# Edge sums of a four-layer graph network: source weights in ScalarE's queue, an earlier folding of the last head's weights, another queue for layer 3's input

## The chip, the cores and the metric

The kernel runs on one NeuronCore of a Trainium2 chip. The metric is the device time of one execution in microseconds. The core has five engines with a queue each: TensorE (PE, matrix products, with its weight loads shown apart as PEld), VectorE (DVE), ScalarE (ACT), GpSimd (POOL) and SyncE (SP, which only issues transfers). Engines wait for each other through semaphores; each works its own queue strictly in order.

## The reference, cut to what matters

The reference is a network of four layers over a graph of 3125 nodes, 256 features each, and 50000 edges. Each layer adds a graph step and a mixer step of the normalized input to x, and then a feed-forward step. Layers 1, 2 and 3 use graph attention; layers 1 and 2 use it twice, with four heads and then with one.

```
def gat_layer(x, src, dst, W, a_src, a_dst, b, heads, out_ch, concat, n):
    h = (x @ W.T).reshape(n, heads, out_ch)
    alpha_src = jnp.sum(h * a_src, axis=-1)
    alpha_dst = jnp.sum(h * a_dst, axis=-1)
    e = jax.nn.leaky_relu(alpha_src[src] + alpha_dst[dst], NEG_SLOPE)
    ...
    out = jax.ops.segment_sum(alpha[:, :, None] * h[src], dst, num_segments=n)
    ...
    return out + b
```

Layer 3 has one attention with four heads of 64; its result is added to the layer's input and to a bias, before an ELU:

```
h_local = jax.nn.elu((agg + x.reshape(n, NH, FOUT)).reshape(n, NH * FOUT) + gat_b)
```

The kernel must compute all of this in float32, the selections of the feed-forward steps (top-k, experts) included.

## The kernel before, in words

**Tiles.** Nodes are cut into 25 tiles of 125 (`NT`, `P`). X, the running activations, stays on chip as 125 x 25 x 256. The edges are a dense matrix of 3125 x 3125 counts in DRAM (`adj`), built at the start; a row tile of it holds the edges of 125 source nodes.

**Edge sums.** `gat_products` runs five times: for the four heads of layer 1 (128 wide), the single last head of layer 1 (256 wide), the four heads of layer 2 (64 wide), its last head (256) and layer 3 (four heads of 64). `h` holds for each source tile and head the features and a one (`width + 1` columns, so that a product gives the sum of the weights too). The exponential of a leaky ReLU of a sum is written as a product of a factor of the source, `gpre`, and a maximum of two factors, `mine` (of the target) and `over` (of the source). So every source row is multiplied once by `gpre` (line 1099): 25 tensor products, of which POOL takes every third. Then the targets' `mine` is spread over the partitions by PE with an identity (`ps_spread`, line 174) and copied to `rows` by DVE (line 78) and ACT (line 80).

For heads of 128 or 256 the loop runs over five groups of five target tiles, and in each over the 25 source tiles `s`: the edges `a` come from `adj` (lines 800 and 801, two transfers issued by SP), DVE makes `t = max(rows, over) * a` for each head (line 1142), and PE multiplies it by `h[:, s]` into PSUM (line 1147). For heads of 64, `sums_by_feature` does the same with four columns of 7, 6, 6 and 6 target tiles; features are on the partitions there (DVE line 1218, PE lines 1223 and 1232), and ACT copies the sums at line 1240. What follows for a target tile is a generator, `use`: it divides by the sum of the weights (`shares`), adds the bias, applies the ELU, and for layers 1 and 2 multiplies by the weights of the last head. `use` runs one group or column behind, stepwise between source tiles.

**The last head's weights.** `gat_heads` loads `W2` (512 x 256 in layer 1, 256 x 256 in layer 2) into `w2a` and the bias into `b1`. `folded` multiplies `w2a` by the attention vectors and sums over features (lines 883 and 884), so that two more columns of `w2a` give the two attention terms of the last head: per layer four transfers on SP, and on DVE 8 + 8 operations in layer 1, 4 + 4 in layer 2. In the order of the program it stands after the layer's mixer, and right ahead of `gat`, whose first step, `gat_spans`, takes the extremes of the attention terms (`ext`, line 1038) and lets PE turn them (`ps_ext`, line 1046). Out of those come `over`, `mine` and `gpre`.

**The layer's input.** `layer_input` normalizes X group by group of four tiles to `XN` (DVE, line 138) and turns it with PE to `XNT`. The mixers read both. In layer 1 SP and ACT also zero two tables in DRAM (`f_rows`, `f_out`) at this time; in layer 2 the last step of the layer before, a gather of the experts' rows by POOL (line 2146) and 50 additions to X by DVE (line 1532), leads up to it. Each mixer begins with an addition of `XN` to X by POOL over the whole array.

**Layer 3.** The layer's input is read from DRAM as `local` (125 x 25 x 256, 3.1 MB) by two transfers issued by ACT (lines 800 and 801). In `l3_local` POOL adds the bias `gat_b` to all of `local` (line 1915), and `use` adds the attention's result to a tile of it (line 1920).

**Order.** A recording layer gathers all operations and orders them by itself before they go to the engines' queues; memory is given out by pools (`with self.pool(...)`), and an operation on a tile whose memory served something else waits for the last user of that memory. So the place of a pool in the program decides both, and a changed pool can move operations of others.

Of the kernel before, what the change touches and what calls it, by code (L numbers as in the profile page):

```python
# [11 lines left out]
F32 = mybir.dt.float32  # L12
BF16 = mybir.dt.bfloat16
I32 = mybir.dt.int32
AF = mybir.ActivationFunctionType
# [45 lines left out]
class Net:  # L61
# [1016 lines left out]
    def gat_products(self, far, h, al, heads, width, loops, use):  # L1078
# [3 lines left out]
        with ExitStack() as es:  # L1082
# [13 lines left out]
            nc.scalar.activation(mine, mine, AF.Exp, scale=-0.8)  # L1096
            for s in range(NT):
                eng = nc.gpsimd if s % 3 == 2 else nc.vector
                eng.tensor_mul(h[:, s], h[:, s], pre[:, s, :, None].to_broadcast([P, heads, width + 1]))
            if width < 96:  # L1100
                self.sums_by_feature(es, mine, over, h, heads, width, loops, use)
                return
# [20 lines left out]
            for g in range(NG):  # L1123
# [10 lines left out]
                for s in range(NT):  # L1134
                    a = ap.tile([P, GW], F32, name="a")
                    self.load_edges(a, self.adj_rows(), s, g)
                    if loops and s // GB == g:
                        blk = a[:, (s % GB) * P:(s % GB + 1) * P]
                        nc.vector.tensor_add(blk, blk, self.ident[:P, :P])
                    t = tp.tile([P, heads, GW], F32, name="t")  # L1140
                    for hd in range(heads):
# [19 lines left out]

    def sums_by_feature(self, es, mine, over, h, heads, width, loops, use):

# [34 lines left out]
        for i0, n in COLUMNS:  # L1198
# [10 lines left out]
            for s in range(NT):  # L1209
                a = ap.tile([P, most], F32, name="a")  # L1210
                self.halves(nc.sync, a[:, :w], self.adj_rows()[s * P:(s + 1) * P, i0 * P:i0 * P + w])
                if loops and i0 <= s < i0 + n:
                    blk = a[:, (s - i0) * P:(s - i0 + 1) * P]
                    nc.vector.tensor_add(blk, blk, self.ident[:P, :P])
                t = []
                for hd in range(heads):
# [84 lines left out]

    def gat_heads(self, prefix, h, al, h2, al2, heads, width, loops, eps):

        nc = self.nc
        wide = heads * width
        chunks = wide // 128
        h2v = h2[:, :, 0, :D]
        with ExitStack() as es:
            wp = es.enter_context(self.pool("tg_w"))
            kp = es.enter_context(self.pool("tg_k", 2))  # L1310
            w2 = wp.tile([128, chunks, D + 2], F32, name="w2a")
            nc.sync.dma_start(w2[:, :, :D], self.ins[prefix + "W2"].rearrange("(c p) m -> p c m", p=128))
            b1 = self.rows(wp, prefix + "b1")
            with self.pool("tg_f") as fp:
                self.folded(fp, w2[:, :, :D], chunks, 1, [prefix + "a_src2", prefix + "a_dst2"],
                            w2[:, :, D:])
            nc.gpsimd.memset(h2[:, :, :, D:D + 1], 1.0)
# [294 lines left out]
    def layer1(self):  # L1612
        self.rows1 = self.dram.tile([MAXB * BLK, D], F32, name="f1_rows")
        self.out1 = self.dram.tile([MAXB * BLK, D], F32, name="f1_out")
        self.blank(self.rows1, MAXB * BLK)
        self.blank(self.out1[OFTEN * BLK:, :], (MAXB - OFTEN) * BLK, 4)
        pre = "L1_gnn_"
        with self.pool("g1_h2") as low:
            last = self.last_terms(low)
            with self.pool("g1_h") as hp:  # L1620
                with self.pool("in1") as ip:
                    xn, xnt = self.layer_input(ip)
                    h, al = self.l1_mix(xn, xnt, lambda: self.gat_project(
                        hp, xnt, pre, "W1", 4, ("a_src1", "a_dst1"), "g1"))
                self.gat_heads(pre, h, al, *last, 4, 128, False, 1e-16)
            self.l1_ffn(lambda xn, xnt: self.gat_last(pre, *last, False, 1e-16, xn, xnt))
# [188 lines left out]
    def layer2(self):  # L1815
        pre = "L2_gnn_"
        with self.pool("g2_h2") as low:
            last = self.last_terms(low)
            with self.pool("g2_h") as hp:
                with self.pool("in2") as ip:  # L1820
                    xn, xnt = self.layer_input(ip)
                    h, al = self.l2_mix(xn, xnt, lambda: self.gat_project(
                        hp, xnt, pre, "W1", 4, ("a_src1", "a_dst1"), "g2"))
                self.gat_heads(pre, h, al, *last, 4, 64, True, 0.0)
            self.l2_ffn(lambda xn, xnt: self.gat_last(pre, *last, True, 0.0, xn, xnt))
# [67 lines left out]
    def l3_local(self, out, h, al, far, flag, most, found):  # L1893
# [4 lines left out]
        with ExitStack() as es:  # L1898
# [15 lines left out]

            nc.gpsimd.tensor_add(out, out, gb[:, None, :].to_broadcast([P, NT, D]))

            def use(pp, i, acc, eps):
                x = kp.tile([P, D], F32, name="agg")
                self.shares(kp, x, acc, 4, 64, less[:, i, :] if eps is None else eps)
                nc.vector.tensor_add(out[:, i, :], out[:, i, :], x)  # L1920
                yield from self.elu(kp, out[:, i, :], "elu")
# [231 lines left out]
    def l3_gnn(self):  # L2153
# [5 lines left out]
        with self.pool("in3_k") as keep:  # L2159
# [414 lines left out]
```

## Time and profile before

| | |
|---|---|
| median of 3 runs | 6754.28 us (6752.83 to 6755.14) |
| the profiled execution | 6747.62 us |
| its span, first to last instruction | 6745.8 us |
| mean granted clock of TensorE | 0.907 |
| DMA over the span | 562 MB, 83 GB/s |

Durations below are of the profiled execution. In a row of a timeline the first number is the start in us from the beginning of the span, the second the busy time; then come engine, line and operation, the tile written and those read, the shape, the number of instructions in the row, and in brackets how long the engine had been idle before it and whose signal came last before it went on. A row with the mark x17 takes 17 neighbouring instructions of one kind together. "PEld" overlaps PE. An engine's name with a q (ACTq, SPq) stands for its issuing of a transfer. A table of waits gives, for an engine's operation and the one that released it, the idle time in all, the number of times and the longest.

The start times of the five edge sums, from the first exponential `gpre` to the first product, are: layer 1's heads 1763.99 to 1782.86, layer 1's last 2437 to 2447.80, layer 2's heads 3726.86 to 3741.30, layer 2's last 4257 to 4267.69, layer 3's 5608.27 to 5617.96.

### The profile page before, as it was taken

The page shows a single profiled execution, that of the slowest core. Times are in us where ns is not written, and L with a number is a line of the kernel's source. Part 1 is how long each engine was busy: PE and PEld are TensorE (multiplying, and loading weights), DVE is VectorE, ACT ScalarE, POOL GpSimd, SP SyncE. Part 2 cuts the span into 40 slices and gives each one's busy share as a digit, 9 for nine tenths or more (in the row PEclk, how much of TensorE's full clock was granted, in tenths as well). Part 3 has the DMA queues.
Part 4 walks back from the last instruction along what each step waited for, and adds up shares of the span by engine and source line. Part 5 has one row for each costly group of instructions (what it writes and reads, how often), then busy time and mean ns, then how long its engine had stood idle before and what let it go on. Part 6 is the DMA issues. An engine that isn't in the chain of part 4 may idle for free. (4 is left out here: it accounts for less than half of the span.)

```text
span 6745.8 us, 78396 instructions
## 1 busy us (share of the span) xinstructions
PE 5820.6 (86%) x29487; PEld 3940.7 (58%) x29487; DVE 3700.8 (55%) x7628; ACT 1599.3 (24%) x3400; POOL 884.5 (13%) x685
## 2 busy tenths in 40 slices
PE   6888899997799989899956899898878887997785
PEld 5555785564699978658844344686534443333553
DVE  7634113215777754215025888546378888886433
ACT  2423002232011110113314011101256561003411
POOL 0000000002200001400031000111324452001101
PEclk7877998998899999889977899998889998998887
DMA  2633447501122234315520222440232223222132
GB/s 67 111 48 61 115 132 219 157 10 57 44 64 63 62 94 134 90 47 171 174 79 9 79 79 77 113 135 1 82 43 62 54 49 94 73 76 68 52 110 76
DMA packets 421342, 562.02 MB, mean 83 GB/s; under 512 B 120485, under 2 KB 307170, under 8 KB 417154
## 3 DMA queue, kind: packets, MB, share of 16 engines
q1 hardware_dynamic: 353687, 458.72, 25.8%
q10 hardware_dynamic: 40467, 70.52, 3.8%
q0 software_dynamic: 26752, 27.20, 1.6%
q8 instruction: 247, 4.05, 0.3%
q14 instruction: 189, 1.54, 0.1%
HBM read 446.41 MB, written 109.65 MB: 82 GB/s over the span
## 5 line engine op out<-in xcount | busy, mean ns | idle before, releaser
L1142 DVE SCALAR_TENSOR_TENSOR t<-rows,over,a 125x625 f32<-125x625 f32 x750 | 619.5, 865 | 423.3 <-PE acc L1147 416.0
L1218 DVE SCALAR_TENSOR_TENSOR t<-rows,over,a 125x750 f32<-125x750 f32 (+1 forms) x800 | 793.9, 1046 | 75.8 <-PE acc L1232 71.0
L1223 PE MATMUL acc<-t,g_h 125*64 125x375 f32 (+1 forms) x3200 | 596.0, 500 | 13.0 <-DVE t L1218 13.0
L1147 PE MATMUL acc<-g_h,t 125*125 125x129 f32 x5000 | 572.4, 274 | 6.3 <-ACT x L1273 3.5
L1147 PE MATMUL acc<-h,t 125*125 125x257 f32 x2500 | 556.7, 382 | 19.5 <-DVE t L1142 9.7
L1147 PEld LDWEIGHTS acc<-g_h,t 125*125 125x125 f32 x5000 | 563.7, 187 | 11.1 <-DVE t L1142 4.3
L1147 PEld LDWEIGHTS acc<-h,t 125*125 125x125 f32 x2500 | 466.2, 188 | 103.1 <-PE acc L1147 18.8
L1223 PEld LDWEIGHTS acc<-t,g_h 125*64 125x64 f32 x3200 | 219.7, 136 | 340.6 <-issue 239.1
L1232 PE MATMUL acc<-t,g_h 125*32 125x375 f32 (+1 forms) x3200 | 359.2, 496 | 0.0
L2093 POOL TENSOR_TENSOR bx<-h,crow 128x500 f32<-128x500 f32 (+1 forms) x224 | 263.7, 1195 | 306.2 <-issue 81.0
L779 PE MATMUL agg<-h,a 125*125 125x257 f32 x1250 | 278.8, 383 | 14.5 <-DMA a<-adj 9.3
L845 DVE SCALAR_TENSOR_TENSOR X<-ps_out,prob,X 125x256 f32<-125x256 f32 x200 | 87.9, 479 | 357.1 <-PE ps_out L166 356.9
L2099 PE MATMUL y<-bx,ident 128*128 128x500 f32 (+1 forms) x448 | 222.2, 610 | 67.4 <-POOL bx L2093 65.4
L779 PEld LDWEIGHTS agg<-h,a 125*125 125x125 f32 x1250 | 234.0, 189 | 57.7 <-issue 18.8
L2090 DVE TENSOR_TENSOR_SCAN h<-da,state,bx 128x500 f32<-128x500 f32 (+1 forms) x224 | 246.2, 1130 | 14.9 <-ACT da L2088 11.5
L569 ACT ACTIVATE h<-ps_hidden,L_ffn_b,bn_s 128x500 f32<-128x500 f32 (+1 forms) x224 | 160.7, 723 | 353.6 <-PE ps_hidden L166 333.5
L1232 PEld LDWEIGHTS acc<-t,g_h 125*32 125x32 f32 x3200 | 99.6, 109 | 237.0 <-issue 236.1
L166 PE MATMUL ps_hidden<-xbt,w 128*128 128x250 f32 x928 | 204.9, 379 | 16.2 <-ACT xbt L151 16.2
L166 PE MATMUL ps_out<-w,hb 128*125 128x256 f32 x928 | 205.0, 379 | 0.0
L166 PEld LDWEIGHTS ps_hidden<-xbt,w 128*128 128x128 f32 x928 | 174.6, 191 | 42.0 <-ACT xbt L151 23.1
L166 PE MATMUL ps_hidden<-XNT,L_ffn_W 128*128 128x500 f32 (+1 forms) x448 | 198.3, 567 | 0.0
L166 PEld LDWEIGHTS ps_out<-w,hb 128*125 128x125 f32 x928 | 174.1, 188 | 25.8
(724 smaller groups left out, 9332.1 us busy)
## 6 DMA issues: line engine op xcount, KB each, us to landing
a<-adj SPq DMA_DIRECT2D x500, 273.4 KB
a<-adj SPq DMA_DIRECT2D x150, 328.1 KB
arow<-adj SPq DMA_DIRECT2D x25, 1367.2 KB
adj<-block SPq DMA_DIRECT2D x22, 1531.2 KB
w<-in_L_ffn_W1p SPq DMA_DIRECT2D x29, 1024.0 KB
w<-in_L_ffn_W2p SPq DMA_DIRECT2D x29, 1024.0 KB
crow<-crows ACTq DMA_DIRECT2D x96, 250.0 KB
a<-adj SPq DMA_DIRECT2D x50, 382.8 KB
```

The source lines that it names most:

```text
L166: self.nc.tensor.matmul(ps, lhsT[k], rhs[k], start=(k == 0), stop=(k == n - 1))
L569: self.nc.scalar.activation(out[:, f, :], ps[:, :nt], func, **kw)
L779: nc.tensor.matmul(acc[b][:P, :D + 1], a[:, b * P:(b + 1) * P], h[:, s, :], start=(s == 0), stop=(s == NT - 1))
L845: nc.vector.scalar_tensor_tensor(x, ps, prob[:, g + j, e:e + 1], x, op0=ALU.mult, op1=ALU.add)
L1142: nc.vector.scalar_tensor_tensor(t[:, hd, :], rows[:, hd, :], over[:, s, hd:hd + 1], a, op0=ALU.max, op1=ALU.mult)
L1147: nc.tensor.matmul(acc(b, hd), t[:, hd, b * P:(b + 1) * P], h[:, s, hd, :], start=(s == 0 and first), stop=(s == NT - 1), skip_group_check ...
L1218: nc.vector.scalar_tensor_tensor(t[hd][:, :w], rows[hd][:, :w], over[:, s, hd:hd + 1], a[:, :w], op0=ALU.max, op1=ALU.mult)
L1223: nc.tensor.matmul(acc[k][c][q * width:(q + 1) * width, :c1 - c0], h[:, s, 2 * k + q, :width], t[2 * k + q][:, c0:c1], start=(s == 0), sto ...
L1232: nc.tensor.matmul(acc[pairs][c][hd * 32:(hd + 1) * 32, :c1 - c0], h[:, s1, hd, width:].to_broadcast([P, 32]), t1[hd][:, c0:c1], start=(s1 ...
L2090: nc.vector.tensor_tensor_scan(h[:, :w], da[:, :w], bx[:, :w], state[:, c, s:s + 1], op0=ALU.mult, op1=ALU.add)
L2093: nc.gpsimd.tensor_mul(bx[:, :w], h[:, :w], crow[:, :w])
L2099: nc.tensor.matmul(acc[c][:, :w], self.ident, terms[c][:, :w], start=(s == 0), stop=(s == S - 1))
```

## The change

Four things are changed.

1. The products by `gpre` are taken from DVE and POOL. A function `weigh(s)` does them for one source tile, head by head, as ACT activations (a copy scaled per partition). It is called in the loop over source tiles, in the first group or column alone, right before the edges are multiplied.
2. Loading and folding the last head's weights is a function of its own, `last_weights`. It is called at the beginning of layers 1 and 2, before `layer_input`, and its tiles live in the pool of `h` (`g1_h`, `g2_h`). In `gat_heads` the pool `tg_w` falls away.
3. `local` of layer 3 is loaded by POOL's queue.
4. The bias of layer 3 is added in `use`, by DVE, to the attention's result of each tile; POOL's addition to all of `local` is gone.

```diff
-            for s in range(NT):
-                eng = nc.gpsimd if s % 3 == 2 else nc.vector
-                eng.tensor_mul(h[:, s], h[:, s], pre[:, s, :, None].to_broadcast([P, heads, width + 1]))
+
+            def weigh(s):
+                for hd in range(heads):
+                    nc.scalar.activation(h[:, s, hd, :], h[:, s, hd, :], AF.Copy, scale=pre[:, s, hd:hd + 1])
             if width < 96:
-                self.sums_by_feature(es, mine, over, h, heads, width, loops, use)
+                self.sums_by_feature(es, mine, over, h, weigh, heads, width, loops, use)
                 return
...
+                    if g == 0:
+                        weigh(s)
                     t = tp.tile([P, heads, GW], F32, name="t")
...
+                if i0 == 0:
+                    weigh(s)
                 t = []
...
-    def gat_heads(self, prefix, h, al, h2, al2, heads, width, loops, eps):
+    def last_weights(self, pool, prefix, wide):
+
+        chunks = wide // 128
+        w2 = pool.tile([128, chunks, D + 2], F32, name="w2a")
+        self.nc.sync.dma_start(w2[:, :, :D], self.ins[prefix + "W2"].rearrange("(c p) m -> p c m", p=128))
+        b1 = self.rows(pool, prefix + "b1")
+        with self.pool("tg_f") as fp:
+            self.folded(fp, w2[:, :, :D], chunks, 1, [prefix + "a_src2", prefix + "a_dst2"], w2[:, :, D:])
+        return w2, b1
+
+    def gat_heads(self, weights, h, al, h2, al2, heads, width, loops, eps):
...
+        w2, b1 = weights
         with ExitStack() as es:
-            wp = es.enter_context(self.pool("tg_w"))
             kp = es.enter_context(self.pool("tg_k", 2))
-            w2 = wp.tile([128, chunks, D + 2], F32, name="w2a")
-            nc.sync.dma_start(w2[:, :, :D], self.ins[prefix + "W2"].rearrange("(c p) m -> p c m", p=128))
-            b1 = self.rows(wp, prefix + "b1")
-            with self.pool("tg_f") as fp:
-                self.folded(fp, w2[:, :, :D], chunks, 1, [prefix + "a_src2", prefix + "a_dst2"],
-                            w2[:, :, D:])
...
             with self.pool("g1_h") as hp:
+                weights = self.last_weights(hp, pre, 512)
                 with self.pool("in1") as ip:
...
-                self.gat_heads(pre, h, al, *last, 4, 128, False, 1e-16)
+                self.gat_heads(weights, h, al, *last, 4, 128, False, 1e-16)
...
             with self.pool("g2_h") as hp:
+                weights = self.last_weights(hp, pre, 256)
                 with self.pool("in2") as ip:
...
-            nc.gpsimd.tensor_add(out, out, gb[:, None, :].to_broadcast([P, NT, D]))
-
             def use(pp, i, acc, eps):
                 x = kp.tile([P, D], F32, name="agg")
                 self.shares(kp, x, acc, 4, 64, less[:, i, :] if eps is None else eps)
+                nc.vector.tensor_add(x, x, gb)
                 nc.vector.tensor_add(out[:, i, :], out[:, i, :], x)
...
-                    self.halves(nc.scalar, local, rows.rearrange(by_tile, p=P))
+                    self.halves(nc.gpsimd, local, rows.rearrange(by_tile, p=P))
```

More of the change, by code (lines that the diff above doesn't have):

```diff
@@ L1160, in gat_products, with sums_by_feature @@
                 advance()
-    def sums_by_feature(self, es, mine, over, h, heads, width, loops, use):
+    def sums_by_feature(self, es, mine, over, h, weigh, heads, width, loops, use):
         nc = self.nc
@@ L1823, in layer2 @@
                         hp, xnt, pre, "W1", 4, ("a_src1", "a_dst1"), "g2"))
-                self.gat_heads(pre, h, al, *last, 4, 64, True, 0.0)
+                self.gat_heads(weights, h, al, *last, 4, 64, True, 0.0)
             self.l2_ffn(lambda xn, xnt: self.gat_last(pre, *last, True, 0.0, xn, xnt))
```

## The prediction

> **What bounds the kernel now.** I read the page's head first, then what TensorE (PE) waits for, then the timelines of the five stretches in which edge sums start, and of the places that the moved work leaves and enters.
>
> ```profile
> span 6745.8 us, 78396 instructions
> ## 1 busy us (share of the span) xinstructions
> PE 5820.6 (86%) x29487; PEld 3940.7 (58%) x29487; DVE 3700.8 (55%) x7628; ACT 1599.3 (24%) x3400; POOL 884.5 (13%) x685
> ```
>
> PE is the bound in most stages, with 925 us of the span idle; ScalarE (ACT) is idle for three quarters. An edit that leaves the matmuls alone, as this one does, can move the time only through PE's idle time. The table of PE's waits (who waits, for whom: us in all, times, longest) shows where that lies:
>
> ```profile
> PE ps_spread L174 <- DVE rows L78: 29.8, 8, 14.9
> ...
> PE ps_spread L174 <- DMA a<-adj: 15.9, 1, 15.9
> ...
> PE acc L1223 <- DVE t L1218: 13.0, 4, 11.9
> PE acc L1147 <- DVE t L1142: 12.4, 14, 5.9
> PE ps_ext L1046 <- DVE ext L1038: 10.9, 1, 10.9
> ```
>
> Each of these is a single long stop at the start of an edge sum. In between, the loop is PE's: from 1790 to 1890 us PE is busy for 99.9 of 100 us, from 2448 to 2500 for 52.0 of 52, from 3742 to 3840 for 98.0 of 98, with a granted clock of 0.97 to 1.00. VectorE (DVE) is busy for 75, 40 and 91% of them. So work taken from DVE inside the loops is worth nothing; work taken from the starts is worth its whole length.
>
> **Weights, layer 1's four heads.** The timelines of DVE, POOL and PE around 1764 us (start, length, group, idle before and who ended it):
>
> ```profile
> 1764.31 17.19 DVE L1099 TENSOR_TENSOR g_h<-g_h,gpre 125x516 f32<-125x516 f32 x17 [0.79 <-ACT gpre L1090]
> 1781.43 0.40 DVE L78 COPY rows<-ps_spread 125x250 f32<-125x250 f32 x1
> ...
> 1764.36 11.74 POOL L1099 TENSOR_TENSOR g_h<-g_h,gpre 125x516 f32<-125x516 f32 x8 [37.16 <-ACT gpre L1090]
> ...
> 1781.89 0.99 PE L174 MATMUL ps_spread<-ident,mine 125*125 125x125 f32 x3 [14.93 <-DVE rows L78]
> 1782.86 1.22 PE L1147 MATMUL acc<-g_h,t 125*125 125x129 f32 x4
> ```
>
> PE had written the first `ps_spread` by 1767.0 (1766.17 + 0.78), but DVE copies it only at 1781.43, behind 17 weightings. Without them the copy starts at 1767.0: 14.4 us. In their place ACT weighs head by head before each source tile. The nearest row is ACT's L1273, 125x128 scaled per partition: 0.358 us; four make 1.43 us per source tile, against PE's 4.43 us per source tile: hidden. If that cover were gone, 25 tiles would cost 36 us. What shows is that the first weighings stand in ACT's order ahead of its own copies of `rows`: in the changed program's order three of them, about 1 us. Gain 13.4.
>
> **The other starts**, by the same reading. Layer 1's last head: 17 weightings from 2437.60 to 2446.23 with PE idle 5.86 and the first sum at 2447.80; PE has spread by about 2440.6, so the first sum comes at about 2440.9: 6.9, less 0.7 for ACT's first weighings (125x257; nearest is L761, 125x256 scaled, 0.472 us): 6.2. Layer 2's heads: copy at 3736.35 that could come at 3729.6: 6.7; there eight weighings precede ACT's first copy. No ACT row has 65 columns: below by L111's 125x4 at 0.20 us, above by the 0.358 of 128 columns; the Trainium skill (ScalarE: Activation LUTs, What ACT_TABLE_LOAD costs) prices one with a pointer operand at about 280 ns + 0.833 ns per element, 334 ns. I take 0.33, so 2.7 us, half of it before PE has spread: 1.5 shows, 5.2 is left. Layer 2's last head (4257.28 to 4265.92, first sum 4267.69): 6.5 less 0.7, 5.8.
>
> **Layer 3's local sums.** Here the queue of ACT and POOL's bias add count too:
>
> ```profile
> 5597.83 9.47 ACTq L801 DMA_DIRECT2D local<-xn  x1
> 5607.35 0.29 ACT L1913 ACTIVATE less<-less 125x100 f32<-125x100 f32 x1 [14.03 <-DMA a<-adj]
> 5608.27 0.29 ACT L1090 ACTIVATE gpre<-over 125x100 f32<-125x100 f32 x1 [0.64 <-DMA a<-adj]
> ...
> 5620.56 14.35 POOL L1915 TENSOR_TENSOR local<-local,L_gnn_gat_b 125x6400 f32<-125x6400 f32 x1 [29.78 <-DMA a<-adj]
> ...
> 5620.27 15.57 DVE L1218 SCALAR_TENSOR_TENSOR t<-rows,over,a 125x875 f32<-125x875 f32 x2
> ...
> 5635.90 3.18 PE L1223 MATMUL acc<-t,g_h 125*64 125x500 f32 x6 [11.94 <-DVE t L1218]
> ```
>
> Issuing `local` holds ACT for 9.5 us, though DVE has `mine` ready at 5599.2; then two L1218, 1.1 us each elsewhere, take 15.6 while POOL adds the bias, and PE stands 11.94. Afterwards the load is POOL's, the bias is added per tile, and `gpre` comes at about 5598.3, `mine` at 5599.5: PE spreads 9.3 earlier, its 1.43 stop for DVE's weightings goes, and so do the 11.94. Sum 22.7. It agrees with layer 2, the same loop without that stall: from `gpre` to the first column's sums 134.9 us (3726.86 to 3861.8), which less 6 of weightings and from 5598.3 ends at about 5727 instead of 5749.5. Less 1 for ACT's weighings, and less 0.7 for the first `a`, which landed 9 us after its issue beside `local`: 21.
>
> Does the load on POOL's software queue hurt? Its 3125 rows are 25 times those of L2146, a gather of 125 rows by POOL at 1.21 us: about 30 us of POOL, which has nothing else, and `local` is first read by `use` after column 0, some 130 us later. Against it speaks the Trainium skill (SBUF — State Buffer, SBUF: two separate sides): descriptors of such a DMA are written by GpSimd, and a DVE operation that holds the shared port locks it out. DVE is busy for 91% of column 0; if only the other 9% of 130 us (12 us) served, some 18 of the 30 us would be left when `use` blocks DVE, and the 21 would shrink to about 3. The row decides: 50 gathers stood between DVE's L1532 operations from 3449 to 3525 at 1.21 us, at most 1.46. But DVE was mostly waiting for them there, so I keep 3 as the lower end, 23 as the upper.
>
> The 25 new adds of 125x256 cost what L1920 shows, 0.42 each with the next 0.34 later. From 5690 PE is busy for 50 of 50 us with DVE at 46: 19 of them lie under PE (all 25 would be 8.5 us without it). The last column's six stand in DVE's closed chain from 6134.65 to 6145: -2.
>
> **The fold leaves its place.**
>
> ```profile
> 1752.43 0.76 DVE L883 TENSOR_TENSOR fold_t<-w2a,fold_a 128x256 f32<-128x256 f32 x2 [4.69 <-DMA fold_a<-in_L_gnn_a_src]
> ...
> 1758.24 2.04 PE L1046 MATMUL ps_ext<-ident,ext 125*125 125x125 f32 x8 [10.95 <-DVE ext L1038]
> ```
>
> In layer 1 DVE's `ext` (1757.85), and everything behind it to `gpre`, waits for four loads issued on SP from 1747.42 (4.69 of idle) and 16 fold operations (5.3 us). Nothing else keeps `ext`: 10.0. In layer 2 the fold (3673.74 to 3676.28) lies under PE's context product, for which DVE then still waits 2.52: nothing, at most 0.5.
>
> **And enters another.** The loads' issues on SP (0.4 us each) now precede the zeroing of `f_rows`, and in DVE's order the fold stands after the last update of X and before the first XN. In layer 1 the load of `w2a` may start after that update: 1600.97, some 4 us to land (as the 4.69), 5.3 of folding, so the first XN at about 1610.5, 9.5 late. Behind it wait PE's turns and ACT. Before, DVE then stood 1.78 for POOL's `sq`, 3.21 for ACT's `li_s` (held by the zeroing transfers until 1627.5), and 2.20 for a load at 1639.90; part of the delay is taken up there. I worked the changed order through by hand with these lengths: last XN about 4 later; between 2 and 9.5: -4. In layer 2, XN was made between the 50 joins of X; now all 25 come after the last join (3529.7), after w2a's landing (3) and eight fold operations (2.9). Eight XN at 0.32 that were already done then are added, against 10.2 us in which DVE waited between 3530 and 3557. Last XN about 3563 instead of 3557.3: -6, between 2 and 10.
>
> **Sum.** 13.4 + 6.2 + 5.2 + 5.8 + 21 + 10 - 2 - 4 - 6 = 49.6 us. The profiled execution took 6747.62 us, 1.8 around its span; it would come to 6698.0. The median of the runs shown is 6754.28, 6.7 above it; the same gain gives 6704.7, and I predict 6705.
>
> **The rivals.**
> First, the fold pays back all it gains: no slack at either input, -9.5 and -10, so 40 us of gain: 6714. For it: DVE is dense around 1610 to 1623; against: its waits listed above. Second, `local` starves on POOL's queue, layer 3 gives 3 instead of 21: 31.6 us, 6723. Third, the starts turn out to be bound by ACT or by `a` and give half (30.6 becomes 15): 6720; against it, eight prefetched `a` halves at 1765 and ACT idle 16.8 there. Fourth, on the other side: the granted clock of PE. Busy for 5820.6 us at a mean of 0.907, PE would eat the whole 49.6 if its matmuls ran 0.85% slower; from 1.1% on (mean below about 0.897) the kernel is slower than before by a measurable amount, say 6770. For it: less idle time at the same work is a denser load. Against it: the rows tie low clocks to idle stretches (0.52 from 1764 to 1790, 1.00 right after). That nothing happens, because PE hides the weights anyway, is excluded by the 14.93.
>
> **Numbers.** A measurement of this kernel tells 0.2% (13.5 us) from no change. Likeliest case 0.58 (6705, own range 6692 to 6718), fold 0.14, local 0.11, half starts 0.05, clock and anything of its size 0.08, near no change 0.04. Every upper end together (layer 3 at 23, inputs at -2 each, the tail at 0, ACT's first weighings free) gives 63.5 us, 6691; 6684 leaves 7 for the clock. To 6742 it covers two of the rivals together. Faster 0.87, same 0.05, slower 0.08.
>
> **What would show it.** No L1099 on DVE or POOL; ACT rows of 125x129, 125x65, 125x257 inside the first groups; the first acc within 5 us of `gpre` at layer 1; PE's wait for `ps_spread` below 5; L1218's 15-us pair gone; `ext` straight behind the last X update; XN of layer 1 about 4, of layer 2 about 6 later. I'm wrong if DVE waits for `local` at the first `use`, if the last XN of either layer comes over 10 late, or if the loops' clock falls.

## The result, and the profile after

| | before | after |
|---|---|---|
| median of 5 runs | 6753.03 us (6746.27 to 6755.14) | 6713.8 us (6699.23 to 6727.26) |
| the profiled execution | 6747.62 us | 6699.23 us |
| its span | 6745.8 us | 6697.4 us |
| mean granted clock of TensorE | 0.907 | 0.911 |

The ratio of the runs is 0.9942 (95% interval 0.9923 to 0.9962). On two other chips the same pair gave 0.9917 (0.9903 to 0.993) and 0.9932 (0.9918 to 0.9945). So the changed kernel is faster by 0.6 to 0.8%, 39 to 58 us, and single runs of it differ by some 16 to 28 us among themselves. The prediction was 6705 us, in a range of 6684 to 6742. The profiled execution after is the fastest of its five: between the profiled executions the gain is 48.4 us, between the medians 39.2.

The page's head of the kernel after. DVE is down by 58.9 us and POOL by 56.5, ACT is up by 95.1. PE's total has hardly moved, but it is a sum of unlike parts: 18.1 us more in three columns of layer 3, and 12.3 less between the first product of layer 1's last head and the last XN of layer 2 (973.1 to 960.8).

```profile
span 6697.4 us, 78870 instructions
## 1 busy us (share of the span) xinstructions
PE 5818.5 (87%) x29487; PEld 3939.7 (59%) x29487; DVE 3641.9 (54%) x7568; ACT 1694.4 (25%) x3750; POOL 828.0 (12%) x646
```

The waits of PE after (who waits, for whom: us in all, times, longest). The 29.8 us for `rows` are down to 1.9, the 11.9-us stop for DVE's `t` to 2.7 and the 10.9 for `ext` to 0.8. What is left at the starts is mostly a wait for `mine` (9.6 us in two times before, 10.2 now).

```profile
PE ps_spread L174 <- ACT mine L1096: 10.2, 2, 5.7
...
PE acc L1151 <- DVE t L1146: 8.1, 14, 1.6
...
PE acc L1229 <- DVE t L1224: 3.4, 3, 2.7
...
PE ps_spread L174 <- DVE rows L78: 1.9, 5, 0.5
...
PE ps_ext L1046 <- DVE ext L1038: 0.8, 1, 0.8
```

The start of layer 1's heads after, from the timeline of all engines. ACT weighs three heads (x3) ahead of its first copy of `rows`, as the prediction said; DVE's copy comes right behind PE, and the first product 4.5 us after `gpre` instead of 18.9.

```profile
1753.88 0.29 ACT L1090 ACTIVATE gpre<-over 125x100 f32<-125x100 f32 x1
...
1754.42 0.97 ACT L1101 ACTIVATE g_h<-g_h,gpre 125x129 f32<-125x129 f32 x3
1754.48 0.96 PE L174 MATMUL ps_spread<-ident,mine 125*125 125x125 f32 x3 [4.52 <-ACT mine L1096]
1755.48 0.47 ACT L80 COPY rows<-ps_spread 125x375 f32<-125x375 f32 x1
...
1756.83 0.42 DVE L78 COPY rows<-ps_spread 125x250 f32<-125x250 f32 x1 [3.38 <-PE ps_spread L174]
...
1758.37 1.23 PE L1151 MATMUL acc<-g_h,t 125*125 125x129 f32 x4
```

The input of layer 1 after, DVE's timeline. The fold stands where the diff puts it, behind the last update of X; the first XN starts 10.5 us after that update instead of 0.4.

```profile
1597.09 0.48 DVE L845 SCALAR_TENSOR_TENSOR X<-ps_out,prob,X 125x256 f32<-125x256 f32 x1 [2.56 <-PE ps_out L166]
1602.17 0.76 DVE L883 TENSOR_TENSOR fold_t<-w2a,fold_a 128x256 f32<-128x256 f32 x2 [4.60 <-DMA L_gnn_b<-in_L_gnn_b]
...
1607.59 2.68 DVE L138 TENSOR_SCALAR XN<-X,li_mv,li_rs 125x256 f32<-125x256 f32 x8
```

And the start of layer 3 after. `local` costs POOL 1.50 + 0.72 us of issuing, `mine` follows at once, and then DVE stands 4.00 us for the first edges.

```profile
5551.57 1.50 POOL L800 DMA_DIRECT2D local<-xn  x1 [6.52 <-SPq L1915]
...
5553.07 0.72 POOL L801 DMA_DIRECT2D local<-xn  x1
5553.12 0.29 ACT L1090 ACTIVATE gpre<-over 125x100 f32<-125x100 f32 x1 [0.93 <-DVE low L1092]
...
5554.04 0.29 ACT L1096 ACTIVATE mine<-mine 125x100 f32<-125x100 f32 x1 [0.63 <-DVE mine L1095]
...
5560.81 1.13 DVE L1224 SCALAR_TENSOR_TENSOR t<-rows,over,a 125x875 f32<-125x875 f32 x1 [4.00 <-DMA a<-adj]
```

**The span cut into stretches.** Each stretch is a difference of two times in the timeline of the one execution: the end of layer 0's last update of X, and otherwise starts (the first product of a layer, the first copy of a column's sums by ACT, and so on; layer 2's last `gpre` before starts at 4256.34). The last column is what the prediction's steps say of it.

| stretch | before | after | difference | predicted |
|---|---|---|---|---|
| to the end of layer 0 (last line 845) | 1601.05 | 1597.57 | -3.5 | 0 |
| layer 1: from there to `gpre` | 162.9 | 156.3 | -6.6 | -6 (+4, -10) |
| layer 1's heads: `gpre` to the first product | 18.9 | 4.5 | -14.4 | -13.4 |
| layer 1's last head: the same | 11.1 | 5.6 | -5.5 | -6.2 |
| from there to layer 2's `gpre` | 1279.1 | 1279.5 | +0.4 | +6 |
| layer 2's heads: `gpre` to the sums of column 0 | 134.9 | 127.0 | -8.0 | -5.2 |
| layer 2, column 1 | 123.8 | 120.8 | -3.0 | 0 |
| layer 2's last head: `gpre` to the first product | 11.4 | 4.3 | -7.1 | -5.8 |
| layer 3: first operation (`less`) to the sums of column 0 | 153.6 | 130.7 | -22.9 | -21 |
| layer 3, columns 1 to 3 | 381.4 | 399.3 | **+17.9** | 0 |
| from there to the end | 614.9 | 617.1 | +2.1 | +2 |
| the three stretches between | | | +2.0 | 0 |
| sum | | | -48.6 | -49.6 |

The differences come to the span's 48.4 but for rounding. The total agrees with the prediction within 1.2 us, yet the largest positive term is one that it had at zero: three columns of layer 3 became 17.9 us longer. It is offset by small gains that were set too low, by one cost that was set too high, and by scatter of unchanged code. So the closeness of the total is in good part luck. A right sum with a wrong term in it needs an explanation as much as a wrong sum, so most of the experiments are about these columns.

The windows of the three columns, before and then after (length; busy time and instructions of PE, PEld, DVE, ACT, POOL; granted clock; DMA's share; GB/s).

```profile
5749.49:5879.99 130.50, 129.88 (x854) 46.47 (x852) 106.15 (x155) 11.61 (x26) 0.00 (x0) 1.00 0.26 73
5879.99:6006.20 126.21, 126.21 (x844) 45.56 (x842) 103.22 (x146) 9.62 (x22) 0.00 (x0) 1.00 0.27 75
6006.20:6130.87 124.67, 124.67 (x835) 44.50 (x833) 101.67 (x144) 8.79 (x21) 0.00 (x0) 1.00 0.23 64
```

```profile
5681.07:5818.39 137.32, 136.89 (x856) 48.46 (x854) 108.00 (x162) 11.71 (x26) 0.00 (x0) 1.00 0.25 69
5818.39:5950.14 131.75, 131.75 (x844) 46.53 (x842) 104.69 (x152) 9.62 (x22) 0.00 (x0) 1.00 0.26 72
5950.14:6080.35 130.21, 130.21 (x835) 45.35 (x833) 104.06 (x150) 8.78 (x20) 0.00 (x0) 1.00 0.22 62
```

PE is busy all the time in both, does the same number of products at the same clock of 1.00, and takes longer. So it neither waits for DVE's added work nor runs slower in clock. DVE is not full: 106 of 130 us before. The groups of the page say which of the products grew: line 1232 (1238 after), the sums of the weights, one product per head into 32 rows of `acc`. Before, and after:

```profile
L1232 PE MATMUL acc<-t,g_h 125*32 125x375 f32 (+1 forms) x3200 | 359.2, 496 | 0.0
```

```profile
L1238 PE MATMUL acc<-t,g_h 125*32 125x375 f32 (+1 forms) x3200 | 374.0, 496 | 0.0
```

The count is 3200 and one of them takes 496 ns in both, but their united time is 14.8 us longer; in the three columns alone it is 17.7 (151.9 before, 169.6 after), nearly all of the 17.9. They overlap one another, and after the change they overlap less. The timeline of PE inside column 1 shows how. A product leaves two records here (1600 products in the code, 3200 instructions), so x2 is one product and x8 four. Before:

```profile
5782.11 0.82 PE L1232 MATMUL acc<-t,g_h 125*32 125x375 f32 x2
5782.86 1.49 PE L1223 MATMUL acc<-t,g_h 125*64 125x375 f32 x8
5784.28 0.84 PE L1232 MATMUL acc<-t,g_h 125*32 125x375 f32 x8
5785.05 1.49 PE L1223 MATMUL acc<-t,g_h 125*64 125x375 f32 x8
5786.47 2.10 PE L1232 MATMUL acc<-t,g_h 125*32 125x375 f32 x22
```

After:

```profile
5731.38 1.49 PE L1229 MATMUL acc<-t,g_h 125*64 125x375 f32 x8
5732.80 1.45 PE L1238 MATMUL acc<-t,g_h 125*32 125x375 f32 x6
5734.18 1.49 PE L1229 MATMUL acc<-t,g_h 125*64 125x375 f32 x8
5735.60 1.46 PE L1238 MATMUL acc<-t,g_h 125*32 125x375 f32 x10
```

Four products, one per head, cost 0.84 us together, and a single one costs 0.82: the four heads write four different sets of 32 rows, and such products run side by side (the four at 5784.28 start within 0.02 us of one another and last 0.50 us each, then their second records follow). Eleven in a row take 2.10. In the lines before, 16 products (1 + 4 + 11) take 3.76 us. After, the planner cuts these eights into 3 and 5, with a head twice in each part, and 16 take twice 1.45 + 1.46, 5.82 us. The starts in the trace show it: of the three, two start together and the third 0.65 us later; of the five, three and then two. Over the three columns there are 13 rows of 3 and 11 of 5 before, 29 and 27 after. A **turn**, one or more products of different heads in a row, costs about 0.64 us (2.10 less 0.82, over two turns more). What counts is the number of turns, and that is set by the order in which the recording layer puts the products on PE's queue. The code that issues the products is the same; the order moved because `use` has one operation more, as the next section shows.

Counted in the order of PE's queue, columns 1 to 3 of layer 3 have 70 + 67 + 67 turns before and 80 + 75 + 75 after: 26 more, 16.6 us at 0.64, against 17.9 measured. The starts in the traces, grouped where more than 0.1 us lies between two of them, give the same counts. (The forecasts below call a turn a slot, and a row of such products a run.)

### The profile page after: what moved, and what is told of

Its sections match the earlier page's. It is cut to its first block, busy times and chain, and to the rows that moved or that the text cites. A ratio compares the mean times of both kernels' runs of the same rounds, so it can differ in the third digit from the quotient of the medians.

```text
span 6697.4 us, 78870 instructions
## 1 busy us (share of the span) xinstructions
PE 5818.5 (87%) x29487; PEld 3939.7 (59%) x29487; DVE 3641.9 (54%) x7568; ACT 1694.4 (25%) x3750; POOL 828.0 (12%) x646
## 5 line engine op out<-in xcount | busy, mean ns | idle before, releaser
L1224 DVE SCALAR_TENSOR_TENSOR t<-rows,over,a 125x750 f32<-125x750 f32 (+1 forms) x800 | 778.2, 1025 | 71.7 <-PE acc L1238 63.8
L1151 PEld LDWEIGHTS acc<-g_h,t 125*125 125x125 f32 x5000 | 565.2, 188 | 10.9 <-DVE t L1146 4.3
L1151 PEld LDWEIGHTS acc<-h,t 125*125 125x125 f32 x2500 | 466.4, 188 | 98.8 <-PE acc L1151 18.9
L1238 PE MATMUL acc<-t,g_h 125*32 125x375 f32 (+1 forms) x3200 | 374.0, 496 | 0.0
L149 PE MATMUL ps_turn<-ident,XN 125*128 125x125 f32 x300 | 58.0, 345 | 158.5 <-DVE XN L138 128.2
```

The source lines that it names most:

```text
L1151: nc.tensor.matmul(acc(b, hd), t[:, hd, b * P:(b + 1) * P], h[:, s, hd, :], start=(s == 0 and first), stop=(s == NT - 1), skip_group_check ...
L1224: nc.vector.scalar_tensor_tensor(t[hd][:, :w], rows[hd][:, :w], over[:, s, hd:hd + 1], a[:, :w], op0=ALU.max, op1=ALU.mult)
L1238: nc.tensor.matmul(acc[pairs][c][hd * 32:(hd + 1) * 32, :c1 - c0], h[:, s1, hd, width:].to_broadcast([P, 32]), t1[hd][:, c0:c1], start=(s1 ...
```

## The experiments

**The changed kernel again.** It is run as it is, beside the next three experiments.

> The changed kernel once more, unchanged. Its five times spread over 28 us where those of the kernel before spread over 9. If that is the kernel's own, five more times spread over 20 us or more again, and this profile differs from the first in a place that can be named; if it was the chip at that hour, they lie within 10 us. Either way the three later columns of layer 3 take 137.3, 131.8 and 130.2 us again (first sums copy to first sums copy), not the 130.5, 126.2 and 124.7 of before.

Measured 6694.93 us beside 6753.06, ratio 0.9917 (0.9903 to 0.993), with the columns at 137.3, 131.8 and 130.2 us. Its five times spread over 16 us, between the two forecasts, so that question stays open. The columns are the same to a tenth of a microsecond in every profile of this kernel; what varies is elsewhere, the end of layer 0 for one (1597.6 to 1601.7 in three profiles of it, though nothing changed there).

**The bias alone.** The kernel before, with part 4 of the change only.

```diff
-            nc.gpsimd.tensor_add(out, out, gb[:, None, :].to_broadcast([P, NT, D]))
-
             def use(pp, i, acc, eps):
...
                 self.shares(kp, x, acc, 4, 64, less[:, i, :] if eps is None else eps)
+                nc.vector.tensor_add(x, x, gb)
```

> The kernel before with the bias of layer 3 per tile in DVE instead of POOL's one add, and nothing else of the change. Theory P (the new add changes the order in which PE gets its products: sums of weights split three and five take two slots of 0.635 us each where one and seven took three in all): columns of layer 3 at 137.3, 131.8, 130.2, PE's stall of 11.94 in column 0 gone, tail +2, so about 8 us slower than before. Rival S (transfers on the software queue, or ACT's weighing, disturb the later columns): columns as before, and the time 10 us faster.

Measured 6758.61 us beside 6753.06, ratio 1.0009 (1.0 to 1.0017): part 4 alone gains nothing, and by its medians costs 5.6 us. The two halves are both in its trace. From `less` to the sums of column 0 it takes 144.4 us instead of 153.6, so PE's stop of 11.94 behind POOL's addition is gone. The start gains some 9 us and not 11.9 because, with that addition gone, POOL's eight weightings run beside DVE's seventeen, which then take 9.25 us (from 5616.32) instead of 5.86 (from 5608.59), and the first product comes 13.1 us after `gpre` instead of 9.7. The columns take 137.6, 131.8 and 130.2, the long ones. The lengthening belongs to this part and to no other.

**The addition elsewhere in `use`.** The changed kernel, with the bias added to `local` ahead of the sums, once without and once with a `yield`:

```diff
             def use(pp, i, acc, eps):
+                nc.vector.tensor_add(out[:, i, :], out[:, i, :], gb)
                 x = kp.tile([P, D], F32, name="agg")
                 self.shares(kp, x, acc, 4, 64, less[:, i, :] if eps is None else eps)
-                nc.vector.tensor_add(x, x, gb)
```

> The changed kernel with the same 25 adds of 125x256 on DVE, but the bias is added to the tile of local ahead of the attention's sums instead of to agg. DVE has the same work; in PE's built order the sums of weights of columns 1 to 3 stand as in the kernel before (70, 67, 67 slots instead of 80, 75, 75). Theory P: columns at 130.5, 126.2, 124.7 again, 17 us faster than the changed kernel. Rival D (DVE's added work itself makes the columns longer): columns stay at 137, 132, 130 and the time stays.

```diff
                 self.shares(kp, x, acc, 4, 64, less[:, i, :] if eps is None else eps)
-                nc.vector.tensor_add(x, x, gb)
+                yield
+                nc.vector.tensor_add(out[:, i, :], out[:, i, :], gb)
```

> The changed kernel with one more step in use: shares first, then (a step later) the bias and the sum. The same DVE work; PE's built order has 64, 63, 63 slots in columns 1 to 3. Theory P: 0.635 per slot and 0.115 per run, so 4, 2.6 and 2.6 us below before's columns: 126.5, 123.6, 122.1, and about 26 us faster than the changed kernel. Rival D: columns stay at 137, 132, 130.

Both have DVE's 25 additions of 125x256, and the columns come out at 130.2, 126.2 and 124.6 in the first, 125.7, 122.6 and 122.1 in the second. That excludes the length of the additions as the cause. The total doesn't show the gain, so the forecasts of 17 and 26 us less both failed: 6709.67 us (ratio 0.9939, 0.9926 to 0.9953) and 6697.64 (0.9917, 0.9904 to 0.9931), beside 6694.93 for the changed kernel. The reason is a new wait, in the timeline of the first of the two at the start of layer 3:

```profile
5580.67 0.43 DVE L1928 TENSOR_TENSOR local<-local,L_gnn_gat_b 125x256 f32<-125x256 f32 x1 [28.70 <-DMA local<-xn]
...
5582.32 0.29 ACT L1096 ACTIVATE mine<-mine 125x100 f32<-125x100 f32 x1 [30.06 <-DVE mine L1095]
...
5582.70 4.91 PE L174 MATMUL ps_spread<-ident,mine 125*125 125x125 f32 x18 [36.48 <-ACT mine L1096]
```

An addition that needs nothing but `local` and the bias can be planned early, and the planner put some of them ahead of DVE's `mine`. There they hold DVE for 28.70 us until `local` has landed; ACT waits for `mine`, and PE stands 36.48. The second shows the same, with 35.1 us from `gpre` to the first product. In the changed kernel the addition needs the sums of its tile, and so can't be drawn forward.

**One `yield` more.** So the next kernel keeps the addition on the sums and changes nothing but its place in the planner's steps:

```diff
                 self.shares(kp, x, acc, 4, 64, less[:, i, :] if eps is None else eps)
+                yield
                 nc.vector.tensor_add(x, x, gb)
```

> The changed kernel with one more step in use: shares first, a step later the bias is added to agg and agg to local. The added bias still needs the attention's sums, so DVE can't be given it ahead of mine, where it waited 29 us for local in the two runs with the bias on local. PE's built order has 66, 65, 65 slots and 42, 40, 40 runs in columns 1 to 3 against 80, 75, 75 and 43, 41, 41 of the changed kernel. Theory P: 34 slots of 0.635 and 3 runs of 0.115 less, 22 us; columns at 128, 125.3 and 123.7 us, the start of layer 3 as in the changed kernel, some 6680 us. Rival D (DVE's added work makes the columns): columns at 137, 132, 130 and no gain.

Measured 6691.13 us beside 6759.57, ratio 0.9905 (0.9889 to 0.9921); the columns take 128.7, 125.8 and 123.6. The same additions on the same engine, and 21.1 us less in the columns. To see whether that reaches the end, both kernels were then run on one chip.

> The changed kernel again, beside the next two on one chip, so that what the order of the weight-sum products costs from end to end is read directly. Theory (order of products): columns 1 to 3 of layer 3 take 137.3, 131.8 and 130.2 us as before, and the time stands about 0.8% under the kernel before. Rival (the columns are offset elsewhere): the time is the same as that of the kernel with the yield, whatever the columns do.

> The changed kernel with one yield ahead of the bias add. Theory: columns 1 to 3 come to 128.7, 125.8 and 123.6 us (399.3 in profiles before, 378.1 now), 21 us less than the changed kernel, and all of it reaches the end: the time is 21 us (0.3%) under the changed kernel on the same chip. Rival: the later work takes the gain back, and the two times agree within 5 us.

The changed kernel took 6697.59 us (6691.64 to 6708.13), the one with the `yield` 6680.19 (6674.86 to 6689.05), beside 6746.62 for the kernel before; the ratios to it are 0.9932 (0.9918 to 0.9945) and 0.9906 (0.9891 to 0.9921). The difference is 17.4 us, and no run of the changed kernel is as fast as the slowest with the `yield`. So the columns' gain reaches the end, within the scatter of the runs. The group of the page and PE's timeline in column 2 show why, in the kernel with the `yield`:

```profile
L1238 PE MATMUL acc<-t,g_h 125*32 125x375 f32 (+1 forms) x3200 | 352.3, 496 | 0.0
```

```profile
5861.89 0.84 PE L1238 MATMUL acc<-t,g_h 125*32 125x375 f32 x8
5862.65 1.49 PE L1229 MATMUL acc<-t,g_h 125*64 125x375 f32 x8
5864.07 0.84 PE L1238 MATMUL acc<-t,g_h 125*32 125x375 f32 x8
...
5866.25 1.46 PE L1238 MATMUL acc<-t,g_h 125*32 125x375 f32 x14
```

The rows are of four and of seven products again, 374.0 us have become 352.3, and of the 3s and 5s six and one are left in the three columns.

**A shorter addition.** Length or count? Here the added operation stays, with one column instead of 256; the bias of the other 255 is left out.

```diff
-                nc.vector.tensor_add(x, x, gb)
+                nc.vector.tensor_add(x[:, :1], x[:, :1], gb[:, :1])
```

> The changed kernel with the added operation of each tile in layer 3 cut down from 256 columns to one (the bias reaches only the first column of the output, the rest of it is left out). Theory (order of products: the planner's turn counts, not the length): with 75, 71 and 71 slots instead of 70, 67 and 67 in the kernel before and 80, 75 and 75 in the changed one, at 0.635 us a slot, columns 1 to 3 take about 133.7, 128.8 and 127.2 us, half way between the two. Rival (the adds load VectorE: 25 x 0.42 us): a one-column add costs almost nothing and the columns return to 130.5, 126.2 and 124.7. Second rival (any extra operation, whatever its length, costs the same): they stay at 137.3, 131.8 and 130.2.

Measured 133.8, 128.9 and 127.4 us against the forecast 133.7, 128.8 and 127.2. Both rivals miss by some 3 us in each column. The time is 6692.80 us (two runs), 4.8 under the changed kernel on the same chip, where the columns give 9.2. All kernels together, with turns counted in PE's order:

| kernel | turns in columns 1 to 3 | the three columns, us | all of line 1232 or 1238, us |
|---|---|---|---|
| addition on `local`, `yield` | 190 | 370.4 | 349.2 |
| `yield` ahead of the addition | 196 | 378.1 | 352.3 |
| before | 204 | 381.4 | 359.2 |
| addition on `local` | 204 | 381.0 | 358.5 |
| one column | 217 | 390.1 | 364.9 |
| changed | 230 | 399.3 | 374.0 |
| bias alone | 231 | 399.6 | 377.5 |

From the first row to the last 41 turns cost 29.2 us, 0.71 us a turn. Of this 27.6 are the weight-sum products themselves (142.6 and 170.3 us in the columns), 0.67 a turn; the rest lies in other rows. That it is a little more than 0.64 may come from the changes to other products and back, of which there are more when rows are cut; this was not shown. Why the planner cuts at 3 and 5 was not looked into; that the length of the operation enters is shown by the 217.

**Weighing alone, fold alone.** The kernel before with part 1 only, and with part 2 only (their diffs are those of the change).

> The kernel before with the weighing on ACT and nothing else. Theory: starts of layer 1's heads 14.2 shorter, of its last head 5.2, of layer 2's heads 8 and 3 in its second column, of its last head 6.6, and about 3 at layer 3, where ACT's issue of local and POOL's add stay: 40 us faster than before. Rival (starts bound by ACT or by the edges): half of it, 20 us.

> The kernel before with the early folding and nothing else. Theory: layer 1's gpre 9.5 earlier after the mixer and 3 later at the input, layer 2's 2.3 earlier and 1 later: 8 us faster. Rival (the input pays all back): no gain.

Weighing alone: 6715.35 us beside 6759.57, ratio 0.9939 (0.9919 to 0.9958), 44 us. Its stretches: layer 1's heads 4.5 us from `gpre` to the first product, its last head 5.8, layer 2's heads 127.1 to the sums of column 0, its last head 4.4: as in the changed kernel. Against before this is 14.4 + 5.3 + 7.8 + 6.9, with 3.0 for layer 2's column 1 (120.8 here too, 123.8 in the kernels without part 1) and 3.3 for layer 3's start: 40.7. Columns 1 to 3 of layer 3 stay at 381.5. So most of the gain, 40.7 of 48.4 by the traces, is this part's. Layer 3's start gains so little here because PE's stop behind POOL's addition stays:

```profile
5596.74 3.18 PE L1229 MATMUL acc<-t,g_h 125*64 125x500 f32 x4 [11.27 <-DVE t L1224]
```

Fold alone: 6749.09 us, ratio 0.9986 (0.9976 to 0.9995), 10.5 us. Layer 1 from the end of layer 0 to `gpre`: 38.9 to the last XN (35.8 before) and 117.9 from there (127.2), 156.8 instead of 162.9. `ext` stands right behind the last update of X:

```profile
1744.92 3.92 DVE L1423 TENSOR_TENSOR X<-X,ps_m 125x256 f32<-125x256 f32 x9
1748.75 0.33 DVE L1038 TENSOR_REDUCE ext<-g_al 125x4 f32<-125x100 f32 x1
```

For layer 2 the trace settles little. From the first product of layer 1's last head to layer 2's `gpre` it is 1279.1, 1275.5 and 1273.4 us in the three kernels with the old place of the fold, and 1272.5 to 1280.6 in ten profiles with the new one ahead of the input: means of 1276.0 and 1278.1. A cost of 6 is not there; anything from -1 to +4 can be.

**`local` back on ACT's queue.** The changed kernel without part 3.

```diff
-                    self.halves(nc.gpsimd, local, rows.rearrange(by_tile, p=P))
+                    self.halves(nc.scalar, local, rows.rearrange(by_tile, p=P))
```

> The changed kernel with local loaded by ACT's queue again. Theory: ACT is held some 9.5 us by the issue, gpre of layer 3 and the first product come 5 to 9 us later, columns unchanged: 5 to 9 us slower than the changed kernel. Rival (the software queue's long landing, 28 us, and its share of the transfer engines delay the first edges just as much): within 2 us of the changed kernel.

Measured 6717.97 us, ratio 0.994 (0.9923 to 0.9957), where the changed kernel has 0.9917, 0.9932 and 0.9942 on three chips: not told apart. In the trace ACT's issue is back and `gpre` is late:

```profile
5569.77 9.74 ACTq L801 DMA_DIRECT2D local<-xn  x1
...
5579.56 0.29 ACT L1925 ACTIVATE less<-less 125x100 f32<-125x100 f32 x1 [14.61 <-DMA a<-adj]
5580.47 0.29 ACT L1090 ACTIVATE gpre<-over 125x100 f32<-125x100 f32 x1 [0.62 <-DMA a<-adj]
```

From DVE's first `less` to `gpre` it is 12.9 us instead of 2.7. But from `less` to the sums of column 0 it is 135.2, where three profiles of the changed kernel have 130.7, 130.7 and 134.1. So the queue is worth 1.1 to 4.5 us there: less than the forecast 5 to 9, and in two of the three profiles more than the rival's 2. Half or more of what `gpre` gains is lost again, because the next thing is late: the first edges. The changed kernel on the third chip shows that wait at its longest for this order:

```profile
5566.54 1.13 DVE L1224 SCALAR_TENSOR_TENSOR t<-rows,over,a 125x875 f32<-125x875 f32 x1 [8.32 <-DMA a<-adj]
5567.72 0.29 PEld L1229 LDWEIGHTS acc<-t,g_h 125*64 125x64 f32 x2 [7.27 <-DVE t L1224]
```

With ACT's queue no row of DVE there waits for `a`: by the time ACT has issued `local` and `mine` follows, the edges are there.

**The fold between input and mix.** Last, the `yield` together with another place for the fold in both layers, to see what the fold's place ahead of the input costs:

```diff
             with self.pool("g1_h") as hp:
-                weights = self.last_weights(hp, pre, 512)
                 with self.pool("in1") as ip:
                     xn, xnt = self.layer_input(ip)
+                    weights = self.last_weights(hp, pre, 512)
```

> The yield, and the fold of both layers moved from ahead of the layer's input to between the input and the mix. Theory (the early fold costs what stands ahead of XN on VectorE): the first XN of layer 1 stands between the last updates of X of layer 0 instead of 10.5 us after them, the fold follows the last XN and lies under TensorE's work, the last XN comes at most 33 us after layer 0's end instead of 38.7, the distance from there to gpre stays at 117.7, and layer 2's input is 2 us shorter; 6 to 12 us in all under the kernel with the yield alone. Rival (the input of layer 1 is bound by the turns and by ScalarE, the fold was hidden): within 3 us of the kernel with the yield alone.

Measured 6656.93 us (6650.52 to 6659.04), ratio 0.9864 (0.9849 to 0.9879), 23.3 us under the kernel with the `yield` alone and the fastest of all. XN came between the updates as forecast; the size was missed, and so was the rest of the way. DVE's timeline of this kernel at the end of layer 0:

```profile
1589.28 1.38 DVE L138 TENSOR_SCALAR XN<-X,li_mv,li_rs 125x256 f32<-125x256 f32 x4
1594.36 0.88 DVE L845 SCALAR_TENSOR_TENSOR X<-ps_out,prob,X 125x256 f32<-125x256 f32 x2 [3.70 <-PE ps_out L166]
...
1599.08 0.48 DVE L845 SCALAR_TENSOR_TENSOR X<-ps_out,prob,X 125x256 f32<-125x256 f32 x1 [0.37 <-PE ps_out L166]
...
1606.76 0.40 DVE L138 TENSOR_SCALAR XN<-X,li_mv,li_rs 125x256 f32<-125x256 f32 x1
1625.01 0.76 DVE L883 TENSOR_TENSOR fold_t<-w2a,fold_a 128x256 f32<-128x256 f32 x2 [16.12 <-DMA f_rows<-zero]
```

XN of layer 1 is made between the last updates of X, which it never was in the kernel before: the last XN comes 7.6 us after layer 0's end instead of 38.8 (at most 33 was expected). Then 8.2 us are given back: the fold waits 16.12 behind the zeroing of `f_rows`, ACT's first copy of `g_h` waits for `fold_t`, and from the last XN to `gpre` it takes 125.8 instead of 117.6. Layer 2 was to gain 2 and loses 5.7 (1282.0 instead of 1276.3). By the traces that is -23.0 for layer 1 and +5.7 for layer 2; the spans differ by 15.8, the medians by 23.3. That memory which XN had to wait for is now given out otherwise is likely, and was not shown.

## Why the prediction was right, and where it was not

**Right.** The weights of layer 1's heads (14.4 for 13.4), of its last head (5.5 for 6.2; 3.7 to 5.5 in three profiles), of layer 2's last head (7.1 for 5.8): a start that waits for a copy behind a block of work on the same engine gains what that block lasts. The fold leaving its place in layer 1 (9.3 to 9.6 for 10.0) and entering the input there (+2.9 for +4). Layer 3's start as a sum (22.9 for 21, 19.4 to 22.9 in three profiles). The tail: from the first sums of the last column to the end of DVE's last operation on `local` 14.6 us became 16.7, +2.1 for +2; that the whole stretch to the end shows the same +2.1 is chance, since it takes 608.6 to 617.0 us in three profiles of the changed kernel.

**Wrong: "An edit that leaves the matmuls alone, as this one does, can move the time only through PE's idle time", and with it "19 of them lie under PE".** The prediction costed the 25 added additions as time on DVE, found PE busy for 50 of 50 us and DVE at 46, and so set the columns' share to nothing. DVE did stay under PE. But an operation added to `use` also moves the order of everything that the recording layer plans beside it, PE's products included, and PE's time depends on that order: 26 turns more, +17.9 us. With PE as the bound, nothing covers that. The bias alone shows it, and the same additions at other places, with 190 to 204 turns, take it away. The prediction read the change in order on DVE and ACT, and took PE's order as given because no product is added or removed.

**Mis-sized, and offsetting it.** Layer 2's heads gave 8.0 to the sums of column 0, not 5.2, and 3.0 more in column 1: the "half of 2.7" that ACT's eight weighings were to show didn't show, and column 1 has four rows of weight-sum products less in PE's order (20 instead of 24) and one turn less, which is some 1 us of the 3.0. By groups of that column the weight sums are 1.4 us shorter and the 64-row products 1.5; why the latter are shorter stays open. Layer 2's input was to cost 6 and, as far as the profiles tell, costs about 2. Layer 0's -3.5 and the +2.0 between are the scatter of unchanged code (layer 0 ends between 1595 and 1607 us in the profiles).

In layer 3 the terms were shifted among themselves: ACT's freed queue was put at 9.3 and the late edges at 0.7, while the edges cost 4.0 and 8.3 in two profiles, so that the queue was worth 1 to 5. The other 18.4 (153.6 to the 135.2 with ACT's queue) came with the weights and the bias, put at 1.43 + 11.94 less 1. The two do not simply add: alone they give 3.3 and some 9, since each alone leaves a stop that the other takes away. And not all that the table of waits was said to show are single long stops: two of its five rows are, the others are 8, 4 and 14 waits, the longest 14.9, 11.9 and 5.9.

**A price that was 14 times too high.** 30 us of POOL for the load's 3125 rows, from the gather of 125 rows at 1.21 us. The load took POOL 2.2 us of issuing, with DVE at work at the time in operations of 0.16 to 0.26 us, and nobody waited for `local`: what the Trainium skill (SBUF — State Buffer, SBUF: two separate sides) made plausible, that a DVE operation holding the shared port shuts POOL's writing of descriptors out, did not show at this place; whether one of these held that port, and what longer DVE operations would do, no run here tells. A gather of 125 rows by an index was the wrong neighbour for a load with a plain pattern.

**The rivals.** That the fold pays all back is excluded by the fold alone (0.9986, 0.9976 to 0.9995). That `local` starves is excluded by the 2.2 us and by the absence of any wait for it in the changed kernel. That the starts give half is excluded by the 34.4 us that the four of them give in weighing alone, against 15. That PE's clock falls is excluded by 0.911 against 0.907.

## What to carry to other kernels

Where a planner orders the work, an operation that costs its own engine nothing can still cost the engine that bounds the kernel, by moving that one's instructions: compare the order on the bounding engine too, even if none of its instructions is touched, and look for rows of short products that were cut. A group whose count and mean stay the same while its busy time grows is the sign of it. And when a total comes out as predicted, cut the span into stretches all the same: here a term of +17.9 us hid behind several small ones, and undoing it was worth 17 us more.

## What the runs showed of the hardware

- Products of four heads into different sets of 32 rows of the output run side by side on PE: four in a row took 0.84 us, one alone 0.82, eleven 2.10. The price is per turn, 0.64 to 0.67 us, not per product.
- A plain load of 125 x 25 x 256 by POOL's queue held POOL for 1.50 + 0.72 us, where the same load by ACT's queue held ACT for 9.3 to 9.7. DVE could go on about 28 us after POOL's issue (5552.5 to 5580.67, in the kernel where DVE waits for it).
- ACT's scaled copy of 65 columns takes 0.338 us, as estimated (0.33), but in a row they overlap: five take 1.29 us, 0.26 each.
